# Late slab passes behind the last row of y, and layer 2 from row tile 6 on, in a four-layer graph network kernel

## The chip, the core and the metric

The kernel runs on one core of a Trainium2 chip. Its time is the device time of one execution in microseconds. The core has TensorE (PE, with its weight loads listed as PEld), VectorE (DVE), ScalarE (ACT) and GpSimd (POOL); SP issues most of the loads and stores, and POOL issues gathers and some stores. Each engine works through its own list of instructions in order and waits where an instruction's input, or the memory that it writes, is not free yet.

## The reference

There are N = 2708 nodes with D = 512 features in `x`, and one matrix `adj` of 2708 × 2708 with few entries that are not zero (most of them in the first rows and columns). Four layers each add something to x; `LN` is a layer norm along the features.

```python
h = relu(LN(x)); mask = adj > 0                      # layer 0
inc = adj + mask / max(sqrt(sum(mask, -1)), 1e-12)
x = x + (inc @ h) / sum(inc, -1)

h = relu(LN(x))                                      # layer 1, 8 heads
a = softmax(q(h) k(h)^T / 8 - 1e16 * (1 - max(adj, eye)))
x = x + sum_heads(a @ v(h) @ Wo)

h = relu(LN(x))                                      # layer 2
u = relu(adj @ (h @ W1) + b1)
u = relu(adj @ (u @ W3) + b3)
x = x + tanh(u @ Wf + bf)

h = relu(LN(x))                                      # layer 3
x = x + (adj != 0) @ (h @ W + b) / sum(adj != 0, 0)
```

The softmax of layer 1 puts all weight on the place of the greatest entry of max(adj, eye) in each row. The kernel therefore computes y = h Wv Wo for every node, finds that place for each row and gathers that row of y; flags tell whether a row needs more than that, in which case another branch would be taken.

## The kernel before

Rows are cut into 22 row tiles of 128 (the last has 20). The first DENSE = 6 tiles of rows and columns of adj are treated as dense; behind them, a row tile m has a list of CHUNKS[m] × 128 columns in which it has entries, found by ranks (`ranks`, `search`) and fetched by gathers (`gather_adj`, `gather_rows`).

**Statistics of a slab.** A slab `ar` is one row tile of adj, 128 × 2708 (1354 KB), in one of three buffers. `stats_to(m)` (L688) loads the slabs in an order, and for each makes its signs (`sgn`), the count of its positive entries, the row's norm `rn` and sum `deg`. A full pass over a slab consists of `count_signs` (L516: two ScalarE activations over the slab, Sign with the sum of the signs and Relu with the count) and `attended` (L555: VectorE writes the diagonal into the slab, then MAX8 and FIND_INDEX8 give the greatest entry `tops` and its place `at_top`). For the tiles in `LATE` the first visit makes only the Sign, and the slab is loaded again later for the full pass:

```python
LATE = FIRST + ZERO          # [3, 4, 5, 0, 1, 2]
```

**Layer 0** is the loop at L780 to L838 over m = 0 to 21: `inc` and `incl` (VectorE) for the next tile, the matmuls `acc` (L792), then `after` (L725) for tiles m−2 and m−1, which are layer 1's part: it transposes `hn` (`pt`, L192), copies it with a relu (`hT`, L193), multiplies by `wvo` (`yacc`, L158), copies to `yo` (L736) and stores it as rows of y. Then the tile's `xt` (L805) and its layer norm `norm` (L173): BATCH_NORM_STATS2, `mv`, `rstd` (L180), `shift` (L183), `hn` (L186). At m = 14 + i the slab of LATE[i] is loaded and at m = 15 + i it has its full pass; a copy of one element (`behind`, L162) puts the pass behind xt of that m. Behind the loop stand the copy of the indices `idx` (L840), `degrees` (L317: 22 small matmuls, for layer 3), the last calls of `after` and `flags` (L260).

**Layer 2** begins at about L865. It opens memory pools in the order `g` (`gp`, slots for x, y and the products, and the parts of the products g_hi, g_lo, g_s), `wsetb` (biases and the split of w3), `ap` and others. Pools of layer 0 have given their memory back by then, and new buffers take it over: whoever writes such a buffer waits for the last user of the memory. `fetch(t)` (L1061) loads a tile's x (SP) and gathers its rows of y (POOL, L1067) into slots, AHEAD = 9 tiles in advance. `first_product(t)` (L1074) adds them (L1079), normalises, transposes (`pt`, L902), splits into parts (`v_hi` L907, `v_lo` L908, `v_s`) and multiplies by W1 in three products (`main`, `agg`, L927 and on); `first_parts(t)` makes g_hi, g_lo and g_s of a product (L197 to L207). For row tile 0, `aggregate` (L970) runs over all 22 tiles in place, which is what makes the products: first the dense tiles 0 to 5, in pieces split in three parts, then `others` (6 to 21). The tiles of order_m after that take dense parts and gathered rows of the stored products (`gg`, L962).

The scheduler of the framework places instructions on each engine by its own costs and by the order in the program; `tc.issue_after(i)` keeps what stands under it behind instruction i.

Of the kernel before, what the change touches and what calls it, by code (L numbers as in the profile page):

```python
# [9 lines left out]
FP = mybir.dt.float32  # L10
FR = mybir.dt.float32r
# [11 lines left out]
P = 128  # L23
# [19 lines left out]
def kernel(  # L43
# [129 lines left out]
    def norm(pool, xt, n, dst, func=AF.Identity):  # L173

        stats = pool.tile([P, nc.vector.BN_STATS_DIM], FP, name="stats")
        nc.vector.bn_stats(stats[:n], xt[:n])
        mv = pool.tile([P, nc.vector.BN_AGGR_DIM], FP, name="mv")
        nc.vector.bn_aggr(mv[:n], stats[:n])  # L178
        rstd = pool.tile([P, 1], FP, name="rstd")
        nc.scalar.activation(rstd[:n], mv[:n, 1:2], AF.Sqrt, bias=eps[:n])  # L180
        nc.vector.reciprocal(rstd[:n], rstd[:n])
        shift = pool.tile([P, 1], FP, name="shift")
        nc.vector.tensor_scalar(  # L183
            shift[:n], mv[:n, 0:1], rstd[:n], -1.0, op0=ALU.mult, op1=ALU.mult
        )
        nc.scalar.activation(dst[:n], xt[:n], func, scale=rstd[:n], bias=shift[:n])  # L186

# [38 lines left out]
    with tc.tile_pool(name="l0_slab", bufs=2) as slabs, tc.tile_pool(  # L226
# [278 lines left out]
        ZERO = list(range(LEAD))  # L505
        LATE = FIRST + ZERO
        masks, row, slab = {}, {}, {}
# [7 lines left out]

        def count_signs(m, last):  # L516

            sgn = slabs.tile([P, N], BF, name="sgn", bufs=GROUP)
            behind(sgn[:1, :1], last)
            nc.scalar.activation(sgn, slab[m], AF.Sign, accum_out=sums_sgn[:, m : m + 1])  # L520
            nc.scalar.activation(sgn, sgn, AF.Relu, accum_out=cnts[:, m : m + 1])
# [194 lines left out]
        def gathers_to(m):  # L716
# [4 lines left out]
            while far[0] <= min(m, near[0] - 1):  # L721
                gather_rows(far[0])
                far[0] += 1

        def after(m, hn):  # L725

# [8 lines left out]
            yo = wp.tile([P, D], FP, name="yo")  # L735
            nc.scalar.copy(yo[:n], yacc[:n])  # L736
            pending.append(
# [42 lines left out]
        for m in range(NT):  # L780
# [27 lines left out]
            hns[m] = wp.tile([P, D], FP, name="hn")  # L808
            norm(wp, xt, n, hns[m])
            store(m, xt)  # L810
# [4 lines left out]

            step = m - (NT - 8)
            if 0 <= step < len(LATE):
                load_slab(LATE[step])
            if 0 < step <= len(LATE):
                count_signs(LATE[step - 1], xt[:1, :1])  # L820
                attended(LATE[step - 1])
            if m + 8 == NT + 1:
# [147 lines left out]
    def aggregate(m, parts, shifted, gd, marked):  # L970
# [18 lines left out]
        for ts in dense if dense_of(m) else []:  # L989
            gs = [parts(t) for t in ts]  # L990
            raw, k = load_piece(m, ts)
            hi, lo, s = (
                ap.tile([P, PIECE, P], FR, name=f"a_{part}") for part in ("hi", "lo", "s")
            )
            d = (slice(0, k), slice(0, len(ts)), slice(0, n))
            if marked:
                mark(ts[0], raw)
            nc.scalar.activation(hi[d], raw, AF.Copy, scale=UP)  # L998
            nc.vector.tensor_tensor(lo[d], raw, hi[d].bitcast(FP), ALU.subtract)  # L999
            nc.vector.scalar_tensor_tensor(  # L1000
                s[d], lo[d].bitcast(FP), SHIFT, hi[d].bitcast(FP), op0=ALU.mult, op1=ALU.add
            )
            for i, t in enumerate(ts):
                ghi, glo, gs_ = gs[i]
                first, last = t == 0, t == DENSE - 1
                for acc, a, b, st, sp in (
                    (main, hi, ghi, first, False),
                    (main, lo, glo, False, last),
                    (mixed, s, gs_, first, False),
                ):  # L1010
                    nc.tensor.matmul(acc[:n], a[:k, i, :n], b[:k], start=st, stop=sp)  # L1011
        if chunks:
            for c, (a, g) in enumerate(chunks):
                nc.tensor.matmul(  # L1014
                    mixed[:n],
                    a,
                    g,
                    start=(c == 0 and not dense_of(m)),
                    stop=(c == len(chunks) - 1),
                )  # L1020
        else:
            for ts in others:
                gs = [shifted(t) for t in ts]
                raw, k = load_piece(m, ts)
                for i, t in enumerate(ts):
                    nc.tensor.matmul(
                        mixed[:n], raw[:, i, :], gs[i][:k], start=False, stop=(t == NT - 1)
                    )
        if marked:
# [16 lines left out]
    def g_parts(t):  # L1046
        return [gp.tile([P, D], FR, name=f"g{part}{t}") for part in ("hi", "lo", "s")]

# [9 lines left out]
    xs, ys, g1, g1p = {}, {}, {}, {}  # L1058
    AHEAD = 9

    def fetch(t):  # L1061

        n = rows(t)
        xs[t] = gp.tile([P, D], FP, name=f"slot{t % AHEAD}")
        nc.sync.dma_start(out=xs[t][:n], in_=x1[t][:n])
        ys[t] = gp.tile([P, D], FP, name=f"slot{AHEAD + t % AHEAD}")
        nc.gpsimd.indirect_dma_start(  # L1067
            out=ys[t][:n],
            out_offset=None,
            in_=y[:, :],  # L1070
            in_offset=bass.IndirectOffsetOnAxis(ap=idx[:n, t : t + 1], axis=0),
        )

    def first_product(t):  # L1074
# [23 lines left out]

    for t in range(min(AHEAD, NT)):
        fetch(t)  # L1100
# [44 lines left out]
    def hidden(t):  # L1145
        if t not in halves:
            n = rows(t)
            ht = gp.tile([P, D], FP, name=f"glo{t}")
            nc.sync.dma_start(out=ht[:n], in_=hid[span(t)])
            halves[t] = split_h(gp.tile([P, D], FR, name=f"ghi{t}"), ht, n)  # L1150
        return halves[t]

    def room():
# [7 lines left out]
        for t in range(1, DENSE):  # L1161
            yield gp.tile([P, D], FP, name=f"gs{t}")
        i = 0
# [93 lines left out]
    def full_steps():  # L1257
# [9 lines left out]
        for ts in dense + others:  # L1267
            k = rows(ts[0])
            pairs = []
            for t in ts:  # L1270
                if t < DENSE:
                    pairs.append(hidden(t))
                else:
                    hi = gp.tile([P, D], FR, name=f"gs{1 + slot % (DENSE - 1)}")
                    slot += 1
# [18 lines left out]
    for m in order_2:  # L1294
# [18 lines left out]
        else:  # L1313

            place = {order_2[-1]: "gs0", NSLOT: f"slot{order_2[-1]}"}.get(m, f"slot{m}")
            xt = x3[m] = gp.tile([P, D], FP, name=place)
        nc.sync.dma_start(out=xt[:n], in_=x2[m][:n])
# [12 lines left out]
        elif m == order_2[-1]:  # L1330

            hi, lo = (gp.tile([P, D], FR, name=f"g{part}{m}") for part in ("hi", "lo"))
            nc.scalar.copy(hi, go)
# [465 lines left out]
```

## Time and profile before

| | us |
|---|---|
| runs | 1393.85, 1397.64, 1398.86 |
| median | 1397.64 |
| profiled execution | 1403.91 |
| its span | 1402.0 |
| TensorE busy in the span | 1274.1 (91%) |
| last acc of layer 0 ends | 441.2 |
| last yo of layer 1 ends | 463.42 |
| first gather of y's rows | 469.62 |
| first transposes of layer 2 | 481.22 |
| first gathers of layer 2's products in use | 597 |

The page of a profile shows one execution: busy time by engine, forty slices of the span with the busy share in tenths, the granted TensorE clock, and the DMA engines' share. The trace behind it has each instruction's start and length, the idle time in front of it and what released it. Layer 0 runs to about 441 us, layer 1's y to 463, the first stage of layer 2 (the products with W1) from 481 to 597.

### The profile page before, as it was taken

The numbers are of one execution on the slowest core, as the hardware profiler recorded it, in microseconds if no ns is written. First come the engines' busy times: TensorE is split into PE (matmuls) and PEld (weight loads), VectorE is DVE, ScalarE is ACT, GpSimd is POOL, SyncE is SP. The second block draws the span as 40 slices with busy tenths as digits, with TensorE's granted clock in tenths as the row PEclk, the third lists the DMA queues.
The fourth block names the chain that finished last, engine by engine and source line by source line (L and its number), as shares of the span: only waits on it lengthen the run. The fifth ranks groups of instructions, "written<-read, shape, count | busy, mean of one in ns | idle before, by whom it ended". The sixth has DMA issues, their size and how long they took to land. (4 is left out here: it accounts for less than half of the span.)

```text
span 1402.0 us, 15500 instructions
## 1 busy us (share of the span) xinstructions
PE 1274.1 (91%) x4478; PEld 768.7 (55%) x4478; DVE 931.4 (66%) x1760; ACT 689.0 (49%) x1051; POOL 655.7 (47%) x702
## 2 busy tenths in 40 slices
PE   4889989979988489999999999899999999978997
PEld 2334434434433267655656666466666666646886
DVE  4787989886997588623434446365566656658786
ACT  5885737733354466413333335244455544546553
POOL 2255677776555311165444441333334344634762
PEclk9999999999999799999999999999999999979999
DMA  9999899998993975487777777856555666748984
GB/s 345 357 325 316 305 327 356 326 336 266 306 341 107 302 251 196 129 276 252 255 210 240 229 230 221 264 172 193 168 166 170 198 203 187 240 146 287 302 279 161
DMA packets 188461, 348.35 MB, mean 248 GB/s; under 512 B 22174, under 2 KB 98868, under 8 KB 184636
## 3 DMA queue, kind: packets, MB, share of 16 engines
q1 hardware_dynamic: 140768, 200.13, 42.6%
q0 software_dynamic: 46032, 145.05, 32.5%
q10 hardware_dynamic: 1568, 2.10, 0.4%
q8 instruction: 37, 0.61, 0.2%
q14 instruction: 56, 0.46, 0.1%
HBM read 284.59 MB, written 62.61 MB: 248 GB/s over the span
## 5 line engine op out<-in xcount | busy, mean ns | idle before, releaser
L1014 PE MATMUL aggs<-gg,ac 128*128 128x512 f32 (+1 forms) x520 | 232.4, 594 | 4.3 <-DMA gg<-g1d,idx_g 4.3
L962 POOL DMA_INDIRECT gg<-g2d,idx_g x130 | 131.0, 1008 | 218.2 <-PE aggs L1014 169.1
L962 POOL DMA_INDIRECT gg<-g1d,idx_g x130 | 133.3, 1025 | 173.7 <-PE aggs L1014 103.7
L792 PE MATMUL acc<-h,inc 128*128 128x512 f32 (+1 forms) x348 | 168.0, 631 | 10.7 <-DVE inc L642 10.7
L573 POOL DMA_INDIRECT ac<-in_adj_t_dram,idx_a x130 | 131.2, 1009 | 93.9 <-issue 32.6
L1014 PEld LDWEIGHTS aggs<-gg,ac 128*128 128x128 f32 (+1 forms) x520 | 97.6, 189 | 111.1 <-issue 101.2
L592 POOL DMA_INDIRECT h<-h0d,idx_g x111 | 114.2, 1028 | 34.9 <-issue 20.7
L998 ACT ACTIVATE a_hi<-raw 128x384 fp32r<-128x384 f32 x84 | 43.6, 520 | 160.6 <-issue 87.2
L1011 PE MATMUL agg<-ghi,a_hi 128*128 128x512 f32 x252 | 115.5, 458 | 3.9 <-ACT a_hi L998 3.6
L792 PEld LDWEIGHTS acc<-h,inc 128*128 128x128 f32 (+1 forms) x348 | 66.8, 201 | 87.8 <-issue 72.7
L1011 PE MATMUL agg<-glo,a_lo 128*128 128x512 f32 x252 | 101.9, 404 | 3.5 <-ACT glo L207 3.5
L1011 PE MATMUL aggs<-gs,a_s 128*128 128x512 f32 x252 | 100.0, 400 | 0.8 <-DVE gs L204 0.7
L792 PE MATMUL acc<-h,incl 128*128 128x512 f32 (+1 forms) x222 | 100.5, 599 | 0.0
L999 DVE TENSOR_TENSOR a_lo<-raw,a_hi 128x384 fp32r<-128x384 f32 x84 | 47.2, 562 | 76.5 <-ACT a_hi L998 49.6
L908 DVE SCALAR_TENSOR_TENSOR v_lo<-pt,v_hi 128x512 fp32r<-128x512 f32 (+1 forms) x88 | 56.6, 664 | 44.9 <-ACT v_hi L907 44.4
L158 PE MATMUL yacc<-wvo,hT 128*128 128x512 f32 (+1 forms) x176 | 82.4, 611 | 1.0 <-ACT hT L193 1.0
L962 POOL DMA_INDIRECT gg<-hidr,idx_h x62 | 63.6, 1026 | 41.8 <-PE aggs L1202 15.7
L889 DVE SCALAR_TENSOR_TENSOR u<-aggs,u 128x512 f32<-128x512 f32 x42 | 28.8, 687 | 77.5 <-PE aggs L1014 75.9
L792 PEld LDWEIGHTS acc<-h,incl 128*128 128x128 f32 (+1 forms) x222 | 42.1, 192 | 52.0 <-issue 49.1
L907 ACT ACTIVATE v_hi<-pt 128x512 fp32r<-128x512 f32 (+1 forms) x88 | 48.6, 578 | 43.7 <-PE pt L902 41.9
L180 ACT ACTIVATE rstd<-mv,eps 128x1 f32<-128x1 f32 x88 | 24.5, 289 | 83.2 <-DVE mv L178 61.1
L562 DVE FIND_INDEX8 at_top<-tops,ar 128x8 uint32<-128x2708 f32 (+1 forms) x22 | 65.3, 2970 | 0.0
(326 smaller groups left out, 2781.7 us busy)
## 6 DMA issues: line engine op xcount, KB each, us to landing
ar<-in_adj_dram SPq DMA_DIRECT2D x27, 1354.0 KB
raw<-in_adj_t_dram SPq DMA_DIRECT2D x122, 192.0 KB
slot<-x SPq DMA_DIRECT2D x41, 256.0 KB
at<-in_adj_t_dram SPq DMA_DIRECT2D x27, 384.0 KB
ranks<-rank_b SPq DMA_DIRECT2D x20, 485.2 KB
ac<-lst SPq DMA_DIRECT2D x16, 384.0 KB
h<-in_x_dram SPq DMA_DIRECT2D x21, 256.0 KB
h0d<-h POOLq DMA_DIRECT2D x21, 256.0 KB, 5.7
```

The source lines that it names most:

```text
L158: nc.tensor.matmul(acc[:n], hT[:, c, :n], w[:, c, :], start=(c == 0), stop=(c == NCD - 1))
L562: nc.vector.max_index(at_top[:n, m, :], tops[:n, m, :], ar[:n])
L573: nc.gpsimd.indirect_dma_start(out=ac[:, c, :n], out_offset=None, in_=adj_units, element_offset=dense_of(m) * P * N + m * P, in_offset=bas ...
L592: nc.gpsimd.indirect_dma_start(out=g, out_offset=None, in_=h0d[:, :], in_offset=bass.IndirectOffsetOnAxis(ap=idx_g[:, m, c : c + 1], axis=0),)
L792: product = nc.tensor.matmul(acc[:n], a, g, start=(i == 0), stop=(i == len(pairs) - 1))
L907: nc.scalar.activation(hi[d], pt[d], AF.Relu, scale=UP)
L908: nc.vector.scalar_tensor_tensor(lo[d], pt[d], 0.0, hi[d].bitcast(FP), op0=ALU.max, op1=ALU.subtract)
L962: nc.gpsimd.indirect_dma_start(out=gs[c], out_offset=None, in_=gd[:, :], in_offset=bass.IndirectOffsetOnAxis(ap=index[:, m, c : c + 1], ax ...
L998: nc.scalar.activation(hi[d], raw, AF.Copy, scale=UP)
L999: nc.vector.tensor_tensor(lo[d], raw, hi[d].bitcast(FP), ALU.subtract)
L1011: nc.tensor.matmul(acc[:n], a[:k, i, :n], b[:k], start=st, stop=sp)
L1014: nc.tensor.matmul(mixed[:n], a, g, start=(c == 0 and not dense_of(m)), stop=(c == len(chunks) - 1),)
```

## The change

- `LATE` loses slab 0: slab 0 has its Relu, MAX8 and FIND_INDEX8 at its first visit, and is loaded once.
- Slabs 3 and 4 keep their places (m = 15 and 16). Slab 5 is loaded at m = 18, 1 at m = 19 and 2 at m = 20. Signs of 5 are counted at m = 19; everything else of 5, 1 and 2 stands in the program behind the last `yo`.
- The copies of one element that ordered the passes go; `issue_after` takes their place.
- The indices of tiles 6 to 21 are copied early, those of tiles 0 to 5 and the flags behind the passes.
- `degrees` moves into the loop, to m = 18.
- Layer 2's pools are laid out in the order `wsetb`, `gq` (the parts of the products) and `gp` (slots and the rest).
- Layer 2's tiles are fetched and multiplied in the order 6 to 21, then 0 to 5. For row tile 0, `others` comes first and the dense part last.

Counted by engine, VectorE has 6 instructions fewer, ScalarE 2 and SP 1 (one slab load); TensorE and POOL have the same number.

```diff
-        LATE = FIRST + ZERO
+        LATE = FIRST + ZERO[1:]
...
-        def count_signs(m, last):
+        def count_signs(m):
             sgn = slabs.tile([P, N], BF, name="sgn", bufs=GROUP)
-            behind(sgn[:1, :1], last)
...
-            nc.scalar.copy(yo[:n], yacc[:n])
+            last_yo[0] = nc.scalar.copy(yo[:n], yacc[:n]).ins
...
-            norm(wp, xt, n, hns[m])
+            last_v, last_s = norm(wp, xt, n, hns[m])
...
-            step = m - (NT - 8)
-            if 0 <= step < len(LATE):
-                load_slab(LATE[step])
-            if 0 < step <= len(LATE):
-                count_signs(LATE[step - 1], xt[:1, :1])
-                attended(LATE[step - 1])
+            if m == NT - 4:
+                degrees()
+            for i, t in enumerate(LATE):
+                if m == (NT - 8 + i if i < 2 else NT - 6 + i):
+                    load_slab(t)
+                if i < 2 and m == NT - 7 + i:
+                    with tc.issue_after(last_v), tc.issue_after(last_s):
+                        count_signs(t)
+                        attended(t)
+                if i == 2 and m == NT - 3:
+                    with tc.issue_after(last_s):
+                        count_signs(t)
...
-        nc.vector.tensor_copy(idx, at_top[:, :, 0])
-        degrees()
+        nc.vector.tensor_copy(idx[:, DENSE:], at_top[:, DENSE:, 0])
         after(NT - 2, None)
         after(NT - 1, hns.pop(NT - 1))
         after(NT - 1, None)
         flush()
-        flags()
+        with tc.issue_after(last_v), tc.issue_after(last_yo[0]):
+            for t in LATE[2:]:
+                if t != LATE[2]:
+                    count_signs(t)
+                attended(t)
+            nc.vector.tensor_copy(idx[:, :DENSE], at_top[:, :DENSE, 0])
+            flags()
...
+    wsetb = short.enter_context(tc.tile_pool(name="wsetb", bufs=1))
+    gq = short.enter_context(tc.tile_pool(name="gq", bufs=1))
     gp = short.enter_context(tc.tile_pool(name="g", bufs=1))
-    wsetb = short.enter_context(tc.tile_pool(name="wsetb", bufs=1))
...
         if chunks:
+            whole_part(True, False)
...
+        elif marked:
+            other_part(True, False)
+            whole_part(False, True)
         else:
+            whole_part(True, False)
+            other_part(False, True)
...
+    order_1 = list(range(DENSE, NT)) + list(range(DENSE))
...
-        if t + AHEAD < NT:
-            fetch(t + AHEAD)
+        for k in order_1[order_1.index(t) + AHEAD :][:1]:
+            fetch(k)
...
-    for t in range(min(AHEAD, NT)):
+    for t in order_1[:AHEAD]:
         fetch(t)
```

`whole_part` and `other_part` hold the two loops that `aggregate` had, with the start and stop marks of the accumulation as arguments. Buffers g_hi, g_lo and g_s, and those of the later layers that share their names, come from `gq` in place of `gp`.

More of the change, by code (lines that the diff above doesn't have):

```diff
@@ L182, in norm @@
         shift = pool.tile([P, 1], FP, name="shift")
-        nc.vector.tensor_scalar(
+        shifted = nc.vector.tensor_scalar(
             shift[:n], mv[:n, 0:1], rstd[:n], -1.0, op0=ALU.mult, op1=ALU.mult
         )
-        nc.scalar.activation(dst[:n], xt[:n], func, scale=rstd[:n], bias=shift[:n])
+        return shifted.ins, nc.scalar.activation(
+            dst[:n], xt[:n], func, scale=rstd[:n], bias=shift[:n]
+        ).ins
     def transpose_relu(psum, hn, n, dst):
@@ L723, in gathers_to @@
                 far[0] += 1
+        last_yo = [None]
         def after(m, hn):
@@ L988, in aggregate, with whole_part @@
                 mark(whole, ac)
[L989 to L1011, printed above, removed]
+        def whole_part(first_part, last_part):
+            for ts in dense if dense_of(m) else []:
+                gs = [parts(t) for t in ts]
+                raw, k = load_piece(m, ts)
+                hi, lo, s = (
+                    ap.tile([P, PIECE, P], FR, name=f"a_{part}") for part in ("hi", "lo", "s")
+                )
+                d = (slice(0, k), slice(0, len(ts)), slice(0, n))
+                if marked:
+                    mark(ts[0], raw)
+                nc.scalar.activation(hi[d], raw, AF.Copy, scale=UP)
+                nc.vector.tensor_tensor(lo[d], raw, hi[d].bitcast(FP), ALU.subtract)
+                nc.vector.scalar_tensor_tensor(
+                    s[d],
+                    lo[d].bitcast(FP),
+                    SHIFT,
+                    hi[d].bitcast(FP),
+                    op0=ALU.mult,
+                    op1=ALU.add,
+                )
+                for i, t in enumerate(ts):
+                    ghi, glo, gs_ = gs[i]
+                    first, last = t == 0, t == DENSE - 1
+                    for acc, a, b, st, sp in (
+                        (main, hi, ghi, first, False),
+                        (main, lo, glo, False, last),
+                        (mixed, s, gs_, first and first_part, last and last_part),
+                    ):
+                        nc.tensor.matmul(acc[:n], a[:k, i, :n], b[:k], start=st, stop=sp)
@@ new lines, in other_part @@
+        def other_part(first_part, last_part):
+            for ts in others:
+                gs = [shifted(t) for t in ts]
+                raw, k = load_piece(m, ts)
+                for i, t in enumerate(ts):
+                    nc.tensor.matmul(
+                        mixed[:n],
+                        raw[:, i, :],
+                        gs[i][:k],
+                        start=first_part and t == DENSE,
+                        stop=last_part and t == NT - 1,
+                    )
@@ L1020, in aggregate @@
                 )
-        else:
[L1022 to L1028, printed above, removed]
+        elif marked:
+            other_part(True, False)
+            whole_part(False, True)
+        else:
+            whole_part(True, False)
+            other_part(False, True)
         if marked:
@@ L1046, in g_parts @@
     def g_parts(t):
-        return [gp.tile([P, D], FR, name=f"g{part}{t}") for part in ("hi", "lo", "s")]
+        return [gq.tile([P, D], FR, name=f"g{part}{t}") for part in ("hi", "lo", "s")]
     def load_bias(src, name):
@@ L1059 @@
     AHEAD = 9
+    order_1 = list(range(DENSE, NT)) + list(range(DENSE))
     def fetch(t):
         n = rows(t)
-        xs[t] = gp.tile([P, D], FP, name=f"slot{t % AHEAD}")
+        i = order_1.index(t) % AHEAD
+        xs[t] = gp.tile([P, D], FP, name=f"slot{i}")
         nc.sync.dma_start(out=xs[t][:n], in_=x1[t][:n])
-        ys[t] = gp.tile([P, D], FP, name=f"slot{AHEAD + t % AHEAD}")
+        ys[t] = gp.tile([P, D], FP, name=f"slot{AHEAD + i}")
         nc.gpsimd.indirect_dma_start(
@@ L1147, in hidden @@
             n = rows(t)
-            ht = gp.tile([P, D], FP, name=f"glo{t}")
+            ht = gq.tile([P, D], FP, name=f"glo{t}")
             nc.sync.dma_start(out=ht[:n], in_=hid[span(t)])
-            halves[t] = split_h(gp.tile([P, D], FR, name=f"ghi{t}"), ht, n)
+            halves[t] = split_h(gq.tile([P, D], FR, name=f"ghi{t}"), ht, n)
         return halves[t]
@@ L1161, in room @@
         for t in range(1, DENSE):
-            yield gp.tile([P, D], FP, name=f"gs{t}")
+            yield gq.tile([P, D], FP, name=f"gs{t}")
         i = 0
@@ L1273, in full_steps @@
                 else:
-                    hi = gp.tile([P, D], FR, name=f"gs{1 + slot % (DENSE - 1)}")
+                    hi = gq.tile([P, D], FR, name=f"gs{1 + slot % (DENSE - 1)}")
                     slot += 1
@@ L1315 @@
             place = {order_2[-1]: "gs0", NSLOT: f"slot{order_2[-1]}"}.get(m, f"slot{m}")
-            xt = x3[m] = gp.tile([P, D], FP, name=place)
+            xt = x3[m] = (gq if place == "gs0" else gp).tile([P, D], FP, name=place)
         nc.sync.dma_start(out=xt[:n], in_=x2[m][:n])
@@ L1330 @@
         elif m == order_2[-1]:
-            hi, lo = (gp.tile([P, D], FR, name=f"g{part}{m}") for part in ("hi", "lo"))
+            hi, lo = (gq.tile([P, D], FR, name=f"g{part}{m}") for part in ("hi", "lo"))
             nc.scalar.copy(hi, go)
```

## The prediction

> **What bounds the kernel now.** I read the page first: the busy shares and the slices.
>
> ```profile
> span 1402.0 us, 15500 instructions
> ...
> PE 1274.1 (91%) x4478; PEld 768.7 (55%) x4478; DVE 931.4 (66%) x1760; ACT 689.0 (49%) x1051; POOL 655.7 (47%) x702
> ...
> PE   4889989979988489999999999899999999978997
> ...
> PEclk9999999999999799999999999999999999979999
> DMA  9999899998993975487777777856555666748984
> ```
>
> TensorE is the bound nearly everywhere. The one long dip that this change touches is slice 14 (about 456 to 491 us, a PE digit of 4 and a clock digit of 7): the step from layer 1 to layer 2. The waits of 455 to 490 us say who is late there (engine, tile, releaser: total, times, longest).
>
> ```profile
> PE pt L902 <- ACT slot L186: 18.4, 1, 18.4
> POOL slot L1067 <- DMA bias<-in_L_gnn_b_dram: 11.3, 1, 11.3
> ...
> DVE slot L1079 <- DMA slot<-y,idx: 7.1, 1, 7.1
> ```
>
> TensorE waits 18.4 us for layer 2's first normalised tile, that for the first gather of y's rows (469.62 us, first sum at 476.26), and that for y's last row. The bias load named in the second line is issued at 464.2; what ended last before it was the last row of y, as the timelines of ScalarE and VectorE show (start, length):
>
> ```profile
> 442.67 2.46 ACT L520 ACTIVATE sgn<-ar 128x2708 bf16<-128x2708 f32 x1 [2.61 <-DVE sgn L164]
> ...
> 445.13 0.28 ACT L180 ACTIVATE rstd<-mv,eps 128x1 f32<-128x1 f32 x1
> ...
> 448.78 0.81 ACT L186 ACTIVATE hn<-xt,shift,rstd 128x512 f32<-128x512 f32 x1 [0.27 <-DVE shift L183]
> ...
> 462.85 0.57 ACT L736 COPY yo<-yacc 20x512 f32<-20x512 f32 x1 [3.74 <-PE yacc L158]
> ```
>
> ```profile
> 445.65 2.98 DVE L561 MAX8 tops<-ar 128x8 f32<-128x2708 f32 x1
> 448.55 0.20 DVE L183 TENSOR_SCALAR shift<-mv,rstd 128x1 f32<-128x1 f32 x1
> ...
> 448.75 2.97 DVE L562 FIND_INDEX8 at_top<-tops,ar 128x8 uint32<-128x2708 f32 x1
> ...
> 476.26 1.36 DVE L1079 TENSOR_TENSOR slot<-slot,slot 128x512 f32<-128x512 f32 x2 [7.07 <-DMA slot<-y,idx]
> ```
>
> The pass over slab 2 lies across tile 20's normalisation: its first Sign holds rstd until 445.13, its MAX8 holds shift until 448.55, its FIND_INDEX8 holds tile 21's until 451.86. So the last rows of y pay for the last slabs. Two more views: the windows (PE, PEld, DVE, ACT and POOL busy, clock, DMA share, GB/s) of the start and of layer 2's first stage, and that stage's waits.
>
> ```profile
> 25.00:50.00 25.00, 19.20 (x60) 7.60 (x56) 17.63 (x55) 21.21 (x36) 5.45 (x10) 0.93 1.04 370
> 50.00:100.00 50.00, 43.25 (x127) 18.03 (x125) 38.80 (x104) 46.43 (x61) 20.04 (x27) 0.99 0.97 336
> ...
> 481.00:597.00 116.00, 104.74 (x436) 74.74 (x437) 89.40 (x200) 66.02 (x126) 20.06 (x18) 0.97 0.63 208
> ```
>
> ```profile
> PE agg L1011 <- ACT glo L207: 3.5, 1, 3.5
> ...
> PE main L927 <- ACT v_hi L907: 2.0, 4, 0.7
> ```
>
> The profiled execution took 1403.91 us (span 1402.0 and 1.9 around it), 6.3 above the median of 1397.64. I sum against the span and carry the difference over to the median.
>
> **Part 1: the tail of layer 1.** The passes of slabs 1 and 2 leave the path to y's last row. With the 7.0 us TensorE stall at 390.1 (rb, ended by the incl product that stood behind a MAX8) the order also changes: incl now comes ahead of that MAX8, but xt(17) still follows it, so pt(17) waits about 4.5 us and rb about 1.65. I take acc(19) to end where it ended, near 420.5. Then acc(20) and acc(21) lose a 0.85 us stall and short waits and end at 433.9 and 439.5 (before: 435.35 and 441.2). Behind them only matmuls are left: the rest of yacc(19) to 442.9; pt and yacc of tile 20, 0.60 + 8 matmuls in 3.60 plus copies, to 447.6; the same for tile 21, to 452.0; its yo, 0.57, to 452.6. Tile 21's hn (xt 0.74, statistics 0.95, rstd 0.29, 0.15, 0.20, hn 0.81 behind 439.5) is ready at 443, in time. The last yo ended at 463.42, so it gains about X = 10.8.
>
> **Part 2: what now stands behind it.** The passes of slabs 1 and 2 come after that yo on ScalarE, as the instruction order shows: Sign, Sign, Relu, Relu. Only when the first Sign has read slab 1 may VectorE mark its diagonal. The chain is Sign 2.5, mark 0.3, MAX8 2.97, mark 0.3, FIND_INDEX8 2.97, MAX8 2.97, FIND_INDEX8 2.97, the index copy 0.16, with handovers 15.5 us in all. In the program as built, all gathers of y wait in order on POOL behind the first one, and that one waits for the copy of the first six tiles' indices and for the last Relu, because its buffer lies partly on the memory of those passes. So the early copy of the other tiles' indices buys nothing, although tile 6 needs only those. The first gather starts at 452.6 + 15.5 = 468.1; before, it was 6.2 behind yo (469.62). The gain is X − 9.3 = 1.5 us, and 9.3 us is the point at which it turns into a loss.
>
> On SP's queue the bias loads now also wait for the last FIND_INDEX8 (they lie on the slabs), and the nine loads of x stand behind them; before, five were issued by 463. These nine (2.36 MB, 6.3 us at the 375 GB/s of 470 to 480) now start with the gathers. First sum 6.6 us behind the first gather as before makes 474.7; if the gather's rows came after all nine loads it would be 481. The queue gives each tile's pair in turn, so I take 475.0, and first transposes 4.96 later at 480.0 against 481.22: −1.2, between −4 and +5. The Trainium skill ("DMA: Bandwidth & Descriptors", Issuing engines are not separate DMA queues) says that loads issued from different engines interleave on the same 16 DMA engines; the 1.02 DMA share of 470 to 480 agrees. By that rule alone, an even interleave of nine loads with nine gathers would cost this step up to half of the nine loads, about 3 us, and the sum would be −1 instead of −4; that is an estimate, and it speaks against the change. The splitting of w3 (4.9 us of VectorE) also moves behind the passes, in front of the first sum, where VectorE waits anyway for the rows (7.1 us); uncovered it costs up to 4.9. POOL's list chain ends before 458 and does not bind. The degree matmuls (22, each 0.03) move into acc(19): +0.6, counted there.
>
> **Part 3: layer 2's first stage.** Row tiles 6 to 21 come first, so the splits of the six dense tiles (glo on ScalarE, gs on VectorE, 1.37 us of VectorE each) leave the beginning, where TensorE waits for them: 7.8 us of idle in 481 to 590, the largest 3.51 at 500.7 (ended by glo), after which four matmuls take 1.96 instead of 1.0 and more follow, about 2 us. Gone: 3.5 + 2 for that gap, and some 3.2 of the waits for v_hi and gs. They come back in part at the end: a dense tile needs 5.3 us of VectorE (3.9 + 1.37) against 4.4 of TensorE, 0.9 for each of six less what VectorE has run ahead, 3 to 4. Net −5, between −8 and 0. What follows, the first gathers of layer 2's first products (wait of 3.2 at 596.8), waits for the last store in either order: 0.
>
> After a long idle TensorE is slow, as its timeline around the stall of part 1 shows:
>
> ```profile
> 387.37 2.74 PE L792 MATMUL acc<-h,inc 128*128 128x512 f32 x6
> 397.10 0.77 PE L629 MATMUL rb<-ident,rn 128*128 128x128 f32 x2 [6.98 <-DVE incl L634]
> 397.65 5.07 PE L792 MATMUL acc<-h,inc 128*128 128x512 f32 x6
> ```
>
> Six matmuls took 5.07 us behind it and 2.74 ahead of it, so 2.3 was lost. I keep these 2.3 by leaving acc(19)'s end unchanged. The Trainium skill ("TensorE: Matmul & The Clock Gate", What's actually happening) puts the half clock behind an idle window of about 3.4 us and the way back at another 3.4 us of work. By it the new 4.5 us wait at pt(17) also pays, about 1.7 us as an estimate, and with that in place of the row's 2.3 the sum would be 0.6 lower.
>
> **Part 4: the start.** Slab 0's MAX8, FIND_INDEX8 and mark (6.2 us of VectorE) and its Relu (2.44 of ScalarE) move to its first visit near 29 us; one load of 1354 KB and one Sign go from the tail. The h0 norms, the first at 24.4 and then every 4 us, come up to 8 us later. VectorE has 7.4 us free and ScalarE 3.8 in 25 to 50, while DMA is full (1.04); in 50 to 100 ScalarE is 93% busy and gives little back. Bounds 0 and 6.2 (all of VectorE's work on the path); I take +2, since the row that it is nearest to is the DMA-bound one.
>
> **Sum.** −1.2 − 5 + 2 = −4.2. Span 1397.8, the profiled execution 1399.7, the median 1393.5.
>
> **Rivals.** (a) The gap closes. Sign and MAX8 of slab 1 could start while yacc still runs, and the rest go with it: each us earlier is a us of time. If the passes shrink to the VectorE chain alone (12.6) and the start is absorbed, −4 − 5 − 0 = −9, with the upper −8 for the stage −12: 1386 to 1389. For it: the MAX8 and FIND_INDEX8 rows add up to 11.9. Against: the order on ScalarE.
>
> (b) Slower: the passes behind yo. Mechanism: 15.5 us of chain in the gap, with X smaller than its 9.3. If tile 20 and 21 gain only X = 4 (the list gathers or slab 5's pass, whose MAX8 and FIND_INDEX8 stand behind shift(21), still hold them), the first gather is 5.3 later; with x's late loads +2, the start +4 and the stage −3 it is +8: 1406. For it: the transition's chain is longer in the program order than before, and the index copy made early is not used. Against: only matmuls are left between acc(21) and yo.
>
> (c) It does not do what it says: the stage's gain comes back in its last six tiles and tail and passes cancel: −1.2 − 1 + 2 = 0, 1397 to 1398, no change.
>
> **How the numbers follow.** A measurement of this kernel tells about 0.5% (7 us) from no change: faster is under 1390.6, slower over 1404.6. My forecast (−4, own range 1389 to 1398) has 0.42, (a) 0.24, (b) 0.24, (c) 0.10. Faster: (a), and a fifth of the forecast's chance, 0.33. Slower: (b) with 0.02 taken from it for a time just under the bound, and 0.02 from a start of +6, 0.24. Same: the rest, 0.43. The range goes from (a)'s lower end with the start absorbed, 1384, to (b) with the start at its upper bound, 1408.
>
> **What would show it.** In the changed profile: the last yo near 452.6 (part 1; if after 457, X fails); the first gather at 15 us or more behind it, and released by DMA or VectorE (part 2); the first layer-2 transpose at 478 to 483; TensorE's idle in the 110 us behind it at 3 us instead of 7.8, with waits in its last six tiles (part 3); acc(0)'s first matmul and TensorE's busy time in 25 to 100 us within 2 of 49.05 and 62.4 (part 4). I am wrong if the first transpose comes after 485, if the start moves by over 5, or if a wait appears in layers 2 and 3 that the new memory layout makes and that I have priced at nothing.

## The result and the profile after

| | before | after |
|---|---|---|
| median of four runs each, us | 1398.25 | 1415.48 (1413.76 to 1419.1) |
| ratio, 95% interval | | 1.012 (1.0094 to 1.0145) |
| profiled execution, its span | 1403.91, 1402.0 | 1414.61, 1412.8 |
| last acc of layer 0 ends | 441.2 | 437.6 |
| last yo of layer 1 ends | 463.42 | 451.31 |
| first gather of y's rows | 469.62 | 467.37 |
| first sum, first transposes of layer 2 | 476.26, 481.22 | 474.04, 480.45 |
| first gathers of layer 2's products in use | 596.79 | 607.52 |

The change makes the kernel 1.2% slower. The profiled execution of before lies 6 us above its median, that of after 1 us below its own, so the two profiles show 10.8 of the 17 us. The page after, to be read against the one of before: the span, the busy shares, and the slices of TensorE, its clock and DMA.

```profile
span 1412.8 us, 15483 instructions
...
PE 1280.2 (91%) x4478; PEld 771.7 (55%) x4478; DVE 932.8 (66%) x1754; ACT 685.6 (49%) x1048; POOL 659.5 (47%) x702
...
PE   4789899989987388899999999899999999969998
...
PEclk9999899999999699999999999999999999989999
```

The dip of slice 14 is still there, one tenth deeper in both digits, and of the three slices behind it (494 to 600 us) all stay at 8, where before two of them had a 9. The waits of 480 to 608 us, layer 2's first stage (engine, tile, releaser: total, times, longest), name two waits that are nothing or nearly nothing in the profile of before (the first line is the transition itself):

```profile
PE pt L917 <- DMA slot<-x: 29.8, 1, 29.8
...
PE aggs L1041 <- DVE go L911: 9.7, 4, 3.6
...
DVE slot L1117 <- DMA slot<-y,idx: 8.6, 3, 3.5
```

VectorE's sums of x and y wait 8.6 us for gathered rows of y (before: 0), and TensorE waits 9.7 us for `go`, a product that VectorE makes (before: 0.2). The windows of that stage, before and after, and of the start after (columns as in the prediction):

```profile
481.22:596.79 115.57, 104.54 (x435) 74.53 (x435) 89.18 (x198) 65.80 (x125) 19.85 (x18) 0.97 0.62 208
```

```profile
480.45:607.52 127.07, 109.55 (x437) 77.15 (x438) 90.54 (x208) 65.76 (x125) 21.91 (x20) 0.94 0.63 211
```

```profile
25.00:50.00 25.00, 20.69 (x63) 8.41 (x62) 19.21 (x46) 19.04 (x30) 3.25 (x6) 0.93 0.89 316
50.00:100.00 50.00, 42.00 (x112) 16.55 (x110) 38.61 (x117) 45.33 (x62) 20.34 (x27) 0.97 0.99 352
```

The stage takes 127.1 us against 115.6: 6.5 more of idle TensorE (17.5 against 11.0) and 5.0 more of busy TensorE at a clock of 0.94 instead of 0.97. First transposes 0.8 earlier, stage 11.5 longer, everything behind it equal (805.3 against 805.2): that is the whole difference of the two profiles. The 0.8 holds two opposite parts: layer 0 ends 3.6 earlier, and from there to the first transposes it is 2.8 longer.

The transition, in the timelines of ScalarE, VectorE and POOL:

```profile
450.74 0.57 ACT L739 COPY yo<-yacc 20x512 f32<-20x512 f32 x1 [3.75 <-issue]
451.22 2.45 ACT L521 ACTIVATE sgn<-ar 128x2708 bf16<-128x2708 f32 x1
...
458.56 2.44 ACT L522 ACTIVATE sgn<-sgn 128x2708 bf16<-128x2708 bf16 x1
```

```profile
463.25 2.97 DVE L563 FIND_INDEX8 at_top<-tops,ar 128x8 uint32<-128x2708 f32 x1
...
466.26 0.17 DVE L859 COPY idx<-at_top 128x6 uint32<-128x6 uint32 x1
...
474.04 0.69 DVE L1117 TENSOR_TENSOR slot<-slot,slot 128x512 f32<-128x512 f32 x1 [1.55 <-DMA slot<-y,idx]
```

```profile
467.37 0.99 POOL L1105 DMA_INDIRECT slot<-y,idx  x1 [17.85 <-ACT wb L199]
```

The last yo comes early, the passes of two slabs follow it, the index copy ends them, and POOL, idle for 17.85 us, starts the first gather 16.1 us behind the end of yo. The profile puts its release down to the first piece of w3's split on ScalarE (466.31), which starts as the index copy runs (466.26); which of the two ended the wait, this row does not say.

### The profile page after: what moved, and what is told of

Its sections match the earlier page's. It is cut to its first block, busy times and chain, and to the rows that moved or that the text cites. A ratio compares the mean times of both kernels' runs of the same rounds, so it can differ in the third digit from the quotient of the medians.

```text
span 1412.8 us, 15483 instructions
## 1 busy us (share of the span) xinstructions
PE 1280.2 (91%) x4478; PEld 771.7 (55%) x4478; DVE 932.8 (66%) x1754; ACT 685.6 (49%) x1048; POOL 659.5 (47%) x702
## 4 chain that ended last, share of the span: by engine, by line
PE 55%; DMA 6%; DVE 3%; ACT 2%; issue 2%; POOL 1%; SPq 0%; DVEq 0%; ACTq 0%; POOLq 0%
PE aggs L1052 14%; PE main L942 9%; PE agg L1033 8%; PE mixed L942 4%; PE aggs L1033 4%; PE aggs L1240 3%; PE agg L1240 3%; PE pt L917 3%; PE aggs L1041 1%; PE pt L1240 1%; DMA raw<-in_adj_t_dram 1%; DMA slot<-y,idx 1%; PE agg L942 1%; DMA glo<-hid 1%; PE main L1240 1%
## 5 line engine op out<-in xcount | busy, mean ns | idle before, releaser
L795 PE MATMUL acc<-h,inc 128*128 128x512 f32 x348 | 165.1, 621 | 10.9 <-DVE inc L643 6.1
L593 POOL DMA_INDIRECT h<-h0d,idx_g x111 | 120.5, 1085 | 37.1 <-issue 20.7
L1033 PE MATMUL agg<-ghi,a_hi 128*128 128x512 f32 x252 | 115.6, 459 | 6.1 <-ACT a_hi L1015 5.0
L795 PEld LDWEIGHTS acc<-h,inc 128*128 128x128 f32 x348 | 64.9, 196 | 88.2 <-issue 67.7
L795 PE MATMUL acc<-h,incl 128*128 128x512 f32 (+1 forms) x222 | 105.0, 621 | 0.0
L562 DVE MAX8 tops<-ar 128x8 f32<-128x2708 f32 (+1 forms) x22 | 65.4, 2974 | 0.0
```

The costliest lines, as they stand in the source:

```text
L562: nc.vector.max(tops[:n, m, :], ar[:n])
L593: nc.gpsimd.indirect_dma_start(out=g, out_offset=None, in_=h0d[:, :], in_offset=bass.IndirectOffsetOnAxis(ap=idx_g[:, m, c : c + 1], axis=0),)
L795: product = nc.tensor.matmul(acc[:n], a, g, start=(i == 0), stop=(i == len(pairs) - 1))
```

## The experiments

I began with two theories. **A**: without the dense splits between, VectorE's list runs the sums of x and y far ahead of the products, so they reach tiles whose rows have not arrived; `go` stands behind the waiting sum and TensorE behind `go`. **B**: the loss is in what stands between the last yo and the first gather (passes, loads of x behind them). A second round added **C**, slab 0's pass at its first visit, and **D**, the new memory layout in the later layers. The table has the ratio to before in runs on the same chip, and from the profile: last acc to first transposes, the stage from there to the first product gathers in use, and the time that sums in that stage waited for their rows (of y alone, but in e4, where 3.4 of the 8.2 us are y's and most of the rest x's). Runs a2, b2, e1b, e5, e5b, s1, s2 and t1 were made on a chip on which before itself took 1466 to 1476 us; the others ran where it takes 1398 to 1401. Ratios hold within a chip, so a comparison of two runs from different chips says less than its intervals.

| run | ratio (interval) | acc to pt | stage | sums wait |
|---|---|---|---|---|
| before | 1 | 40.0 | 115.6 | 0 |
| after | 1.012 (1.0094 to 1.0145) | 42.8 | 127.1 | 8.6 |
| e1 old order in layer 2 | 1.011 (1.0055 to 1.0164) | 43.2 | 117.4 | 0 |
| e2 new order only | 1.0014 (0.9983 to 1.0045) | 42.9 | 123.2 | 8.3 |
| e3 after, sums paced | 1.0047 (1.0021 to 1.0072) | 42.8 | 115.4 | 0 |
| e4 free gathers | 1.0139 (1.0086 to 1.0193) | 45.0 | 121.7 | 8.2 |
| b2 before again | one run | 40.4 | 114.9 | 0 |
| a2 after again | 1.0088 (1.0051 to 1.0126) | 42.9 | 126.0 | 8.0 |
| e1b as e1 | 1.0084 (1.005 to 1.0119) | 43.1 | 119.5 | 0 |
| t1 e1 with the old memory | 1.0024 (0.999 to 1.0057) | 44.2 | 117.7 | 0 |
| s1 slab 0 first, alone | 0.9963 (0.9931 to 0.9996) | 38.2 | 116.5 | 0 |
| s2 new memory, alone | 1.0004 (0.9965 to 1.0042) | 40.2 | 112.8 | 0 |
| f4 s1 and s2 together | 1.0012 (0.9988 to 1.0036) | 37.9 | 116.5 | 0 |
| f1 new order, sums paced | 0.9929 (0.9904 to 0.9953) | 39.7 | 111.2 | 0 |
| f2 before, sums paced | 0.999 (0.9966 to 1.0015) | 41.2 | 114.8 | 0 |
| g1 f1 with slab 0 first | 0.9953 (0.9922 to 0.9983) | 37.8 | 114.6 | 0 |
| e5 free gathers mended, paced | 0.9854 (0.9787 to 0.9921) | 34.2 | 117.4 | 0 |
| e5b as e5 | 0.9916 (0.9882 to 0.9951) | 34.2 | 116.9 | 0 |
| e5c as e5 | 0.9968 (0.9944 to 0.9993) | 34.2 | 118.4 | 0 |
| e6 as e5, sums not paced | 0.998 (0.9954 to 1.0007) | 34.2 | 121.4 | 6.5 |

### The order of layer 2: e1, e2, e3, f1, f2

e1 undoes the order in the changed kernel; e2 does the order alone in the kernel before (with `whole_part`, `other_part` and slots by place in the order, as in the change).

```diff
 # e1, against after
-        elif marked:
-            other_part(True, False)
-            whole_part(False, True)
...
-    order_1 = list(range(DENSE, NT)) + list(range(DENSE))
+    order_1 = list(range(NT))
```

> The changed kernel with the old order of layer 2 (row tiles 0 to 21, for row tile 0 the dense part first); the late passes, the new memory and slab 0's first visit stay. Theory A (the order is the loss: without the dense tiles' splits in between, VectorE's list has the sums of x and y up to nine tiles ahead of the products, so it waits for gathers while TensorE waits for the products): the stage from the first layer-2 transpose to the first use of gathered products takes about 116 us as before (127 in the changed kernel) and the kernel 1400 to 1405. Theory B (the late loads are the loss: x, y's gathers and the biases start together behind the passes and the stage runs on late rows whatever its order): the stage stays above 124 us and the kernel at 1412 to 1417.

> The kernel before with the new order of layer 2 alone (tiles 6 to 21 first, the dense part of row tile 0 last); tail, memory and slab 0 as before. Theory A: the stage takes 125 to 128 us and the kernel 1407 to 1412. Theory B: the loads are as early as they were, so the stage takes 111 to 117 us and the kernel 1393 to 1399.

In the profile theory A is right: the waits of the sums are in e2 (8.3 us) and after (8.6), and in e1 they are gone; the stage is 123.2 and 127.1 with the new order, 117.4 with the old. In total time the order is nearly nothing: e2 1.0014, and e1 is as slow as after, then and again on another chip (e1b 1.0084, a2 1.0088). Part of the stage's loss comes back before layer 2 ends: counted from the first transposes, e2 is 7.6 us behind before at the stage's end and 4.6 at the last store of the second products, and a2 is 6.5 behind e1b at the first of these places and level with it at the second (403.2 both). So the cause of the 17 us had to be sought elsewhere too.

e3 takes the waits away without touching the order: a sum is issued behind the product four places before it.

```diff
+    PACE, made = 4, []
...
-        nc.vector.tensor_add(xt[:n], xt[:n], hn[:n])
+        p = order_1.index(t)
+        with ExitStack() as held:
+            if p >= PACE:
+                held.enter_context(tc.issue_after(made[p - PACE]))
+            nc.vector.tensor_add(xt[:n], xt[:n], hn[:n])
...
-        sum_banks_scaled(go, main, mixed, n)     # returns its add now
+        made.append(sum_banks_scaled(go, main, mixed, n))
```

> The changed kernel with each sum of x and y placed on VectorE behind the product of four tiles earlier, so that four sums at most are ahead of a product in place of up to nine. Theory A, with the sums' place as its mechanism: VectorE's waits for gathers in the stage (8.6 us) and TensorE's for products (9.7) go, the stage takes 117 to 120 us and the kernel 1404 to 1409. If the order loses by something else (the two buffers of go, or the late loads), nothing moves: 1412 to 1417.

The stage falls to 115.4, both waits are gone, and 0.7% of the time comes back. The mechanism, in VectorE's and TensorE's timelines of after:

```profile
513.52 0.70 DVE L1117 TENSOR_TENSOR slot<-slot,slot 128x512 f32<-128x512 f32 x1 [3.53 <-DMA slot<-y,idx]
...
514.75 0.67 DVE L911 TENSOR_TENSOR go<-aggs,go 128x512 f32<-128x512 f32 x1
```

```profile
515.47 1.99 PE L1041 MATMUL aggs<-go,raw 128*128 128x512 f32 x2 [3.59 <-DVE go L911]
516.48 2.67 PE L942 MATMUL main<-wa,v_hi 128*128 128x512 f32 x4
...
524.08 1.02 PE L1041 MATMUL aggs<-go,raw 128*128 128x512 f32 x2
524.93 1.20 PE L942 MATMUL main<-wa,v_hi 128*128 128x512 f32 x4
...
532.55 2.01 PE L1041 MATMUL aggs<-go,raw 128*128 128x512 f32 x2 [3.27 <-DVE go L911]
533.58 2.66 PE L942 MATMUL agg<-wa,v_hi 128*128 128x512 f32 x4
```

The sum at 513.52 waits 3.53 us for its rows. The sixth `go` stands behind it, and TensorE waits 3.59 us for that `go`, then runs at half speed: 1.99 instead of 1.02, 2.67 instead of 1.20. Up to this sixth product VectorE's list has 15 sums, where before it had 8; with the pacing, in f1 below, it has 9. A sum so far ahead meets a gather that has only just started, because that in turn waited for a slot: POOL issued the gather of this sum's rows at 507.17, after 5.07 us of waiting, 6.35 us ahead of the sum. POOL's waits of the stage list 27.6 us in four waits of `slot`, ended by `v_hi`.

f1 puts the pacing on e2, f2 on before.

> The kernel before with the new order of layer 2 and paced sums; tail, memory, slab 0 as before. If the place of the sums is all that the new order loses by: VectorE waits for no gather in the stage, the stage takes 111 to 115 us (123.2 with the order alone) and the ratio to before is 0.993 to 0.999, which is the gain that the forecast had put on the order. If the new order loses by something else as well, the stage stays over 117 and the ratio at 1.000 or more.

> The kernel before with paced sums and nothing else. Its VectorE never waits for a gather in the stage, so by theory A pacing has nothing to mend: 0.998 to 1.002, stage 114 to 117. If pacing is a gain by itself: 0.995 or less.

```profile
470.69:581.89 111.20, 106.38 (x438) 75.44 (x439) 91.26 (x197) 66.64 (x124) 21.52 (x21) 0.96 0.67 224
```

This is the stage's window of f1. The stage takes 111.2, which is 4.4 less than before and close to the 5 that I had forecast, and the kernel is 0.7% (10 us) faster than before. The profile places only the 4.4 in what the edit touches: the spans differ by 17.6 us, but 10.2 of them lie in layer 0, whose instruction lists are the same in both. The pacing alone does nothing (f2, 0.999). What the waits cost in total time comes out of the pairs with and without pacing: from e2 to f1 the stage falls by 12.0 us and the ratio by 0.0085 (11.9 us), from after to e3 by 11.7 us and 0.0073 (10.2 us). The order is worth its gain only when the sums are held back; unheld, it is cancelled.

### The transition: e4, e5, e6

e4 frees the gathers: separate pools for slabs and for blocks in layer 0, so that the first slots don't lie on a slab's memory; `idx_d`, a buffer of its own for the indices of tiles 0 to 5; the biases loaded behind the first six x.

```diff
+    idx_d = const.tile([P, DENSE], U32, name="idx_d")
...
-                ac = slabs.tile([P, NCL, P], FP, name="ac", bufs=3)
+                ac = blocks_p.tile([P, NCL, P], FP, name="ac", bufs=3)   # ranks, at, inc, incl too
...
-            nc.vector.tensor_copy(idx[:, :DENSE], at_top[:, :DENSE, 0])
+            nc.vector.tensor_copy(idx_d, at_top[:, :DENSE, 0])
...
+    gy = short.enter_context(tc.tile_pool(name="gy", bufs=1))      # slots 0 to 5 and 9 to 14
```

> The changed kernel with layer 0's slabs and its gathered blocks in two pools, the first six pairs of slots for x and y alone on the second one's memory, the indices of tiles 0 to 5 in a buffer of their own, and the biases loaded behind the first six rows of x. The first gathers wait for y's last row and no longer for the passes. Both theories: first gather at about 455 us in place of 467, first layer-2 transpose at 469 to 472 in place of 480. Theory A: the stage behind it stays near 127 us, so the kernel is 8 to 11 us faster than the changed one, 1404 to 1408. Theory B: the rows are early now, the stage falls to 114 to 118 as well and the kernel to 1392 to 1398.

A miss. The first gather came at 458.66, 8.7 us earlier, but the first transposes at 480.45 as in after. Two things stood in the way. The loads of x, now free to go early, stood in SP's queue ahead of y's stores and waited for slots; so the last yo waited 10.21 us for its own buffer, as ScalarE's timeline of e4 shows:

```profile
455.05 0.57 ACT L742 COPY yo<-yacc 20x512 f32<-20x512 f32 x1 [10.21 <-DMA y<-yo]
```

And the split of w3 (VectorE, 471.86 to 476.8) stood between the first sum and the first norm. e5 mends both and has the pacing; e6 is e5 without pacing.

```diff
 # e5, against e4
+        with tc.issue_after(stored[-1]):                 # the last store of y
+            load = nc.sync.dma_start(out=xs[t][:n], in_=x1[t][:n]).ins
...
+        if p == 9:
+            with tc.issue_after(made[-1]), tc.issue_after(scaled[-1]):
+                split_w3()
+    PACE, made = 4, []                                   # e6: PACE = NT
```

> The version with free gathers, mended in three places that its profile shows (the loads of x stood on SP ahead of y's last rows and held yo's buffer by 10.2 us; the split of w3 stood on VectorE between the first sum and its statistics, 4.9 us) and with the paced sums: x's loads behind y's last store, the split of w3 behind the tenth product, each sum behind the product of four tiles earlier. Theory A with free gathers: first gather near 454 us, first layer-2 transpose at 468 to 472, stage 115 to 119, kernel 1389 to 1396, at or below the kernel before. If the stage only moves forward to wait for its own late rows, it takes 125 and the kernel stays at 1400 or more.

> The version with free gathers and paced sums, again: 0.980 to 0.992 of before as on the slower chip, with the first layer-2 transpose some 10 us earlier than before and the stage at 115 to 119 us.

> The version with free gathers, x's loads behind y and w3's split later, without the pacing. First transpose 8 to 10 us earlier than in the kernel before, as in the paced version. Theory A: the stage is at 121 to 126 us in place of 117 and the ratio 0.995 to 1.002; if the free gathers alone make the gain: 0.984 to 0.992 as in the paced version.

> The version with free gathers and paced sums beside it: 0.985 to 0.992, with 34 us from the last acc to the first transpose and the stage at 115 to 118.

The first gather now follows the end of the last yo by 2.6 to 2.9 us (in e5c by 2.6: 452.72 and 450.13), and the first transposes are 34.2 us behind the last acc in all four, 8.6 less than in after. e5 is faster than before in all three sets of runs, on two chips, by 1.5, 0.8 and 0.3%, the last less than the 0.8 to 1.5% that I had expected; e6, with 6.5 us of waiting sums back, ran on another chip and is the same as before (0.998), which is too near to e5c's 0.9968 to tell the pacing's part here. Theory B holds for the transition of after: it is as long as what the gathers wait for. In e5c the rows are no longer what is late: VectorE takes the first sum without a wait at 461.95, as soon as a MAX8 of the late passes ends, and the first norm at 466.96, behind their last FIND_INDEX8 (462.63 to 465.61). And f1, with no late passes and a transition of 39.7, is as fast as e5c with 34.2: e5c's gain there is lost in its stage (118.4 against 111.2) and behind it (806.3 against 802.5).

### Slab 0, memory, and the late passes: b2, a2, e1b, s1, s2, t1, f4, g1

s1 has slab 0's full pass at its first visit and nothing else, s2 only the order of the pools; f4 is both. t1 is e1 with the old pools, g1 is f1 with s1's edit. b2, a2 and e1b are before, after and e1 on the slower chip; b2 was to show where the first profile of before lies above its median, and on that chip it cannot.

```diff
 # s1, against before
-        LATE = FIRST + ZERO
+        LATE = FIRST + [None] + ZERO[1:]
```

> The kernel before once more, for a second profiled execution. Its 19 runs so far have a median of 1397.6 and the execution profiled first took 1403.9, so some 6 us of it are not in the usual run. If they lie in layer 0 (theory C: slab 0's work at its first visit costs the changed kernel more than the first profiles show), the last acc ends at 434 to 437 here and not at 441; if they lie in layers 2 and 3 (theory D, with the new memory), the part behind the first use of gathered products takes 799 to 802 us and not 805; if they are spread, both move by under 3.

> The kernel before with slab 0's Relu, MAX8 and FIND_INDEX8 at its first visit and its second load gone, all else in its place (slabs 1 and 2 still have their passes at m = 19 and 20). Theory C: the h0 norms and with them layer 0 come later by 4 to 8 us, the kernel is at 1402 to 1406. By the forecast's step it is +2 or less, 1396 to 1400.

> The kernel before with layer 2's memory laid out as in the changed kernel and nothing else. The biases and the split of w3 now lie on the slabs and wait, on SP in front of four of x's loads, for the last FIND_INDEX8, which here ends at 452, ahead of y's last row. Theory D: something in the later layers waits for the new neighbours, 1401 to 1406. Otherwise the time stays within 2 us of before, 1396 to 1400.

> The changed kernel again, on the chip and beside the runs that the next three share, so that ratios to before can be compared: 1.009 to 1.015 as on record. Theory A alone would make the ratio of this run over the next one (old order of layer 2) 1.006 to 1.009.

> The changed kernel with the old order of layer 2, again: its first ratio, 1.011 with an interval of 1.0055 to 1.0164, says that the order is not all, its first profile (stage 117.4, first transpose 480.15) that it is nearly all. If late passes and late loads cost by themselves (theory B): 1.005 or more. If not: 1.000 to 1.004.

> The changed kernel with the old order of layer 2 and the old memory: late passes and slab 0's first visit alone. Theory B with the passes as its cause: same as the run before this (ratio 1.005 or more). Theory B with the memory's waits as its cause (biases in front of x's loads on SP): 0.997 to 1.002.

> The kernel before with slab 0's first visit and the new memory together, but slabs 1 and 2 with their passes in the loop at m = 19 and 20, and the old order of layer 2: what the run with the old order has, without the passes behind the last yo. If these passes are the cause of that run's 0.8 to 1.1%: 0.994 to 1.001, and from the last acc to the first layer-2 transpose 40 us as before and not 43. If slab 0 and memory cost together what neither costs alone: 1.005 or more.

> New order of layer 2, paced sums and slab 0's first visit; passes of slabs 1 and 2 in the loop, old memory. The paced order alone was at 0.993 of before; with the 0.2 to 0.4% of slab 0: 0.989 to 0.993. If slab 0's gain was chance, 0.992 to 0.995. Stage 110 to 112 us, 38 to 40 us from the last acc to the first transpose.

Slab 0 first is a small gain by itself (0.9963): it takes 2 us off the transition. On top of f1 it adds nothing that can be measured (g1 0.9953 against f1 0.9929, where I had expected 0.989 to 0.993), and why g1's stage is 114.6 instead of f1's 111.2 is open. f4 has all of e1 but the late passes: 1.0012 against e1's 1.011 and 1.0084. With the old pools the step from s1 to t1 is 0.6%. So a loss of 0.6 to 1%, or 8 to 14 us, belongs to the late passes with what was moved along with them (degrees, the early index copy). The profiles locate 5 to 6 us of it: last acc to first transposes is 42.8 to 44.2 with late passes (after, a2, e1, e1b, e3, t1) and 37.8 to 38.2 with slab 0 first and the others in the loop. The 42.9 of e2 is another case: there the first gather starts 9.5 us behind the last yo instead of 6.2, in f1, with the same passes, 5.4. The rest stays open.

The memory alone is nothing in total time (s2), yet beside the other edits the kernels with the new pools are 0.5 to 0.6% slower than those without (f4 to s1, on different chips, and e1b to t1; these intervals touch or overlap). Their profiles show one effect of it, without any wait: the same matmuls take longer. This is one group of matmuls in b2 and in s2, which differ in the pools only (busy us, mean ns of one, idle us ahead of them):

```profile
L1202 PE MATMUL pt<-glo,a_lo 128*128 128x512 f32 x12 | 4.7, 389 | 0.0
```

```profile
L1203 PE MATMUL pt<-glo,a_lo 128*128 128x512 f32 x12 | 4.7, 392 | 0.0
```

This group takes 389 ns in all eight profiles with the old pools, before included, and 392 in all twelve with the new ones, on every chip. A stretch of layers 2 and 3 where TensorE never rests, in f1 (old pools) and after (new), both at a granted clock of 1.00 and with 517 matmuls each, of which 515 are the same:

```profile
986.40:1119.10 132.70, 132.60 (x517) 91.52 (x516) 86.07 (x161) 66.13 (x100) 49.87 (x50) 1.00 0.58 185
```

```profile
1012.50:1145.90 133.40, 133.28 (x517) 91.75 (x516) 86.30 (x161) 65.67 (x99) 49.65 (x50) 1.00 0.58 183
```

That is 0.5%. The ends of matmuls are modelled in a profile, so I also went by starts: 500 matmuls of this stretch, the same ones in each profile, take 126.96 to 127.00 us in all eight profiles with the old pools and 127.59 to 127.93 in all twelve with the new ones, on every chip (b2 126.98, s2 127.64). From the last store of the second products to the end, the five kernels with the old pools on the chips where before takes 1398 us need 527.7 to 531.0, the seven with the new ones 531.6 to 536.2, means 529.9 and 534.1: about 4 us. On the slower chip single profiles do not order themselves so (s2 540.2, b2 543.2). Why a matmul is slower with its operands at other addresses, no run here shows.

## Why the prediction was wrong, step by step

Two steps failed: part 2, the transition, forecast at −1.2 us and 2.8 longer from the last acc, and part 3, the stage, forecast at −5 and 11.5 longer. A third cost, the new layout, stood at nothing.

**Part 1 was right in its times.** The last yo ends at 451.31 (forecast 452.6), acc(19) to acc(21) come a little earlier than forecast (437.6 for 439.5), and pt(17) and rb wait 3.35 and 1.63 us (forecast 4.5 and 1.65). Behind them six matmuls took 5.16 us, against 5.07 behind the 6.98 of before, so the 2.3 that I left in the sum stayed in it. But of the 12.1 us by which yo is earlier, 3.6 is the end of acc, and this is not the change's: e2, f1 and f2, with the layer 0 of before, instruction by instruction, ended it at 437.6, 431.0 and 434.9. From the end of acc the yo gains 8.6.

**Part 2 failed in the size of its gain.** The order of the chain was right, and its 15.5 us measured 16.1. Against the 6.2 of before the break-even is then 9.9, and 8.6 is below it. The forecast stood there too: counted from the end of acc it had yo gain 9.1, against a break-even of 9.3, and its 1.5 us were the earlier acc. In t1, with the old pools, the gather is 15.8 us behind yo as well, so the new layout is not needed to hold it there. From the first gather to the first transposes I had 11.9, nearly that of before (11.6); it was 13.1. The first sum came 6.7 us behind the gather (forecast 6.9), the late loads of x and the split of w3 notwithstanding, but then VectorE took the sum of the second tile, which waited 1.37 us for its rows (476.11), ahead of the first norm. Measured from the last acc, I forecast 40.5 for 40.0; it was 42.8, and in a2 42.9. So the mechanism of rival (b), late passes with X below their break-even, is what happened; it was priced for X = 4. In total time the late passes cost 8 to 14 us by ratios, more than the 5 to 6 that the profiles place; where the rest lies stays open.

**Part 3 is the step that failed by its sign.** I took away the waits for glo and gs and put nothing in their place. But in VectorE's list the splits that went had been holding back the sums behind them. Forecast −5, measured +11.5 in the stage; with the sums held, −4.4 (f1). In total time the order alone came to +0.14% (e2, +2 us), since part of the stage's loss comes back behind it. I read who waited for VectorE, and not what VectorE would do with the time it was given. The half speed behind a wait, which I had priced at 2 us for the removed gap, came back behind the new ones. The Trainium skill ("TensorE: Matmul & The Clock Gate", What's actually happening) puts the threshold at about 3.4 us of idle; here a wait of 3.27 us, with 0.60 us of transposes ahead of it, was enough: four matmuls behind it took 2.66 us instead of 1.20.

**Part 4 was too high.** xt(0) came 7.4 us late (89.64 for 82.27), as the upper bound had it, but the delay is gone by xt(3) (153.85 for 153.52); acc(0) began at 48.0, and TensorE is busy for 62.7 us in 25 to 100 against 62.4. Forecast +2; by its ratio s1 alone gains 0.4%, some 5 us. Single profiles cannot tell here, since the end of layer 0 differs by up to 10.2 us among profiles with the same lists.

**What I priced at nothing.** The new layout was to be wrong if a wait appeared in layers 2 and 3. None did, but matmuls took 0.5 to 0.8% longer, some 4 us behind the second products in the profiles.

By ratios: order 0, slab 0 −0.4%, late passes with or without memory +0.6 to +1%, memory 0 to +0.6%; they make up the 0.9 to 1.2% of after, with part of the late passes' and of the memory's share not located in any profile. The order's 0 is a gain of some 10 us (f1) and a loss of 10 to 12: with the waits of the sums gone, after would be at 1.0047 (e3).

## What to carry to other kernels

Work that you take off an in-order engine is also a brake on what stands behind it: list what that engine will do next, and ask whether the inputs of that are there. Judge a shorter path against a fixed point of the same execution (here the last acc), not against the span's start, and a stage's gain against runs, not one profile. Where work is moved to a later place, undo first the buffers and the queue places that tie its consumers to it: e5 did, and f1 shows that a good order needs a bound on how far ahead its producers run; both are faster than before.

## What I had not expected of the hardware

The same kernel took 1398 us on some chips and 1466 to 1476 on another; there the last acc of layer 0 ended at 485.0 instead of 441.2, and what lies behind the stage took 824.5 instead of 805.2. On one chip before ranged from 1390 to 1404 us in 19 runs, more than most effects here, and in single profiles with the same instruction lists of layer 0 (before, e2, f1, f2) its last acc ended between 431.0 and 441.2. And a change of addresses alone moved a matmul's time from 389 to 392 ns at a granted clock of 1.00.
